# A chain of four modulated convolutions: the last quad's products done in column halves, the row ends' last step on GpSimd, and two steps of VectorE moved in quad 0

## The chip, the cores and the metric

The kernel runs on one core of a Trainium2 chip. The core has TensorE (PE, matrix products into PSUM), VectorE (DVE), ScalarE (ACT), GpSimd (POOL) and SyncE (SP, which here only issues DMAs). The metric is the device time of one launch in microseconds (us). The profile is that of one execution. Its times run from that execution's first instruction, and `L767` is line 767 of the kernel's file.

## The reference

`x` is 128 rows of 64 channels by 1024 positions, and each row has a style vector of 128 numbers. The result is `x` plus four convolutions of three taps in a row (same, upsample with blur, same, downsample with blur), whose weights are modulated and demodulated per row. Cut to what matters:

```python
def _layer(x, style, w, b, mw, mb, typ):
    s = style @ mw.T + mb
    weight = SCALE * w * s[:, None, :, None]
    demod = lax.rsqrt(jnp.sum(weight * weight, axis=(2, 3)) + EPS)
    weight = weight * demod[:, :, None, None]
    if typ == 'same':
        out = jax.vmap(_conv_same)(x, weight) + b[None, :, None]
    elif typ == 'upsample':
        out = jax.vmap(_conv_up)(x, weight.transpose(0, 2, 1, 3)) + b[None, :, None]
        out = _blur(out, 2.0 * blur_k, (1, 1))
    elif typ == 'downsample':
        xb = _blur(x, blur_k, (2, 2))
        out = jax.vmap(_conv_down)(xb, weight) + b[None, :, None]
    return out

out = x
for i, typ in enumerate(('same', 'upsample', 'same', 'downsample')):
    out = _layer(out, style, weights[i], biases[i], mod_w[i], mod_b[i], typ)
return x + out
```

All is float32.

## The kernel before

Away from the ends of a row the four layers and the residual are one linear filter of nine taps, and the kernel builds that filter for every row. Rows are taken four at a time, a **quad**; there are 32 quads, 0 to 31. The 128 partitions hold two rows of 64 channels, and a tile's second axis of two holds the two pairs, so every product on TensorE is a 64x64 weight block against 64 rows of data, four such blocks side by side in the array. A float32 product is issued as two instructions, so that one "product" of a quad below is 3 taps x 4 blocks x 2 = 24 matmul instructions of 340 columns.

For a quad, the weights go through three stages on TensorE (`scale3`, `stage1`, `stage2`, `stage3`; PSUM tiles `psS`, `psR`, `psW`), each copied out with a scale, mostly by ScalarE. The result is `Wf`, with nine taps. The data are cut into three planes, since three neighbouring outputs are computed together by a fast algorithm: five products m0 to m4 in place of nine. VectorE makes three weight sums `H` (`combine_a`: h1, the residual's two small steps at L673, h3; `combine_b`: h2, h1 and h2 once more), and the five data sums `T` (`in_g01` and `in_g2` first make `G`; then `in3` at L725 gives T3, `in1` L740 and `in2` L745 give T12, `in04` L754 gives T04). From quad 1's turn on, `in1` and `in2` of a quad mostly run on GpSimd.

The products add up in PSUM. `conv3` starts the accumulator `psA` with m3; ScalarE copies it out (`copy_m3`, L806); `conv1` adds m1; VectorE forms `y1 = 2*psA + m3` (`sum1`, L676); `conv2` adds m2; `sum2` writes `Y = 3*m3 + psA` into the PSUM tile `Y` (L676) and subtracts psA from y1 (L826); `conv4` adds m4 on top of `Y`; `conv0` adds m0 to psA. The three output planes are psA (0), y1 (1) and Y (2), each times a scale `td` per row and channel, plus a constant `tb` (`output`, L844 on ScalarE, L846 on VectorE). Each plane of 340 columns is stored by a DMA of 170 KB for each pair (L849).

The order of all work is written out by hand: each engine runs its instructions in the order of the program text and waits only for data or for a buffer. Quads 0 to 3 are taken by `early_turn`, 4 to 28 by `turn_of`, and 29, 30 and 31 by straight code at L1509 to L1577. In a turn for quad q the weights of quad q+2 and the data sums of q+1 and q+2 are made beside the products of q and q+1.

The first and last three outputs of each row don't follow the filter. They are worked out in some twenty small steps scattered over the turns into the tile `Oe` (128 partitions x 128 rows x 3). Its last step is `rest3_bias` (L1122): bias and the row's own ends from `Xe` added by VectorE, in two halves of the partitions, in the code of quads 30 and 31, each half followed by a DMA.

Of the kernel before, what the change touches and what calls it, by code (L numbers as in the profile page):

```python
# [63 lines left out]
def kernel(  # L64
# [202 lines left out]
    def var_newton(bs, ls=slice(0, NL)):  # L267

        newton(var[:, ls, bs], dm[:, ls, bs], nw[:, ls, bs])
# [371 lines left out]
    def stage3(q, part, pool=None, engs=(nc_a, nc_a)):  # L641

        t = chain[q]
        ps = unit(pool or ps_w, f"psW{q}_{part}")
        if part == 0:
            new_w(q)
        kinds = ((0, 1), (2,))[part]
        n = 0
        for i, kind in enumerate(kinds):
            for k in range(K):  # L650
                gs = [g for g in range(K) if 0 <= K * g + kind - k < 7]
                lo, m = gs[0], len(gs)
                first = K * lo + kind - k
                n += 1
                step = len(kinds)
                at = slice(i + step * lo, i + step * (lo + m - 1) + 1, step)
                same_row(
                    blocks(ps, at),
                    w0s[kind][:, k, :],
                    t,  # L660
                    slice(first, first + K * (m - 1) + 1, K),
                    n == 1,
                    n == K * len(kinds),
                )
        stage3_out(q, ps, *((3, 6), (0, 3))[part], engs)
        return ps
# [24 lines left out]
    def combine_b(q, steps=range(3)):  # L691

        a, b, c, h1, h2, h3 = taps(q)
        plan = (h2, c, -0.5, a), (h1, b, -3.0, h2, ALU.subtract), (h2, h2, -1.0 / 3.0, b)
        for i in steps:
            sum_of(*plan[i])
# [25 lines left out]
    def in3(q, pairs=BOTH_PAIRS):  # L722
        if q < NQ:
            X, t = Xs[q % NX], t_tile(q, "T3")
            nc_v.tensor_sub(t[:, pairs, 0, :NJ], plane(X, 3, pairs), plane(X, 1, pairs))  # L725
# [16 lines left out]
    def in2(q, eng):  # L742
        if q < NQ:
            t, g = t_tile(q, "T12"), Gs[q]
            eng.tensor_sub(t[:, :, 1, :NJ], plane(g, 2), plane(g, 1))  # L745

    def in04(q, pairs=BOTH_PAIRS):
        if q < NQ:
            t, g = t_tile(q, "T04"), Gs[q]
            a, b = g[:, pairs, :NJ], g[:, pairs, 2 * PL : 2 * PL + NJ]  # L750
            both = lambda v, step: bass.AP(
                v.tensor, v.offset, [*(list(d) for d in v.ap[:-1]), [step, 2], [1, NJ]]
            )
            nc_v.tensor_sub(t[:, pairs, :, :NJ], both(a, PL), both(b, 1))  # L754

    def product(q, m, ps, groups=range(K)):

        W, H_ = Wq[q]
        tag, i = SLOT[m]
        for g in groups:  # L760
            for s, rows in enumerate(HALF):
                for c, cols in enumerate(HALF):
                    if m in (0, 4):
                        w = W[rows, tap(m // 2, g), c, :]
                    else:
                        w = H_[rows, m - 1, g, c, :]
                    nc.tensor.matmul(  # L767
                        ps[s][cols, :NB],
                        w,
                        Ts[q, tag][rows, c, i, g : g + NB],  # L770
                        start=(g == 0 and m == 3),
                        stop=(g == K - 1),
                        skip_group_check=True,
                    )
# [21 lines left out]
    def conv3(q, pool=None):  # L796
        if pool:
            A[q] = unit(pool, f"psA{q}")
        elif q not in A:
            open_a(q)  # L800
        product(q, 3, banks(q))

    def copy_m3(q):
        m3c[q] = m_tile("m3", q)
        for s, a in parts(q):
            nc_a.copy(m3c[q][:, s], a)  # L806
# [10 lines left out]
    def conv2(q, *groups):  # L817
        product(q, 2, banks(q), groups or range(K))
# [9 lines left out]
    def conv4(q, *groups):  # L828
        product(q, 4, Y_banks, groups or range(K))
# [286 lines left out]
                op1=ALU.mult,  # L1116
            )

    def rest3_bias(half):

        rows, xs = ((T, slice(1, 4)), (Bo, slice(4, 7)))[half]
        nc_v.scalar_tensor_tensor(  # L1122
            Oe[rows], Oe[rows], bb[rows, 3:4], Xe[rows, :, xs], op0=ALU.add, op1=ALU.add
        )
        nc.sync.dma_start(out_ends[rows], Oe[rows].rearrange("c b j -> c (b j)"))


    PART = slice(0, 16), slice(16, 32), slice(32, B)
# [200 lines left out]
    def outputs(q, i):  # L1329
        for r in range(2):  # L1330
            output(q, i, r)
            if late(q):
                store(q, r, slice(i, i + 1))

    def early_turn(q):
        n, c, s = q + 1, q + 2, q + 3 + (q >= AHEAD)
        twice = q == AHEAD
        if q == 1:
            nc.sync.dma_start(Xe, x_ends)
        stage2(c)  # L1340
        sum2(q)
        if q == 0:
            in_g01(n)
        if q == 1:
            in_g2(n)
            load(n + NX)
        combine_a(n)
        combine_b(n)
        if q == 0:
            in_g2(n)  # L1350
            load(n + NX)
        conv4(q)
        if q == 0:
            var_matmul(PART[1], var_of(PART[1]), start=False)
            var_root(PART[1], var_of(PART[1]))
            in1(n, nc_v)
            in2(n, nc_v)
            var_newton(PART[1])
            table_A(PART[1], dm[:, 2, PART[1]])
            for of in (table_C, vector_c0, table_3, vector_Da):  # L1360
                of(PART[1])
        if q == 1:
            in1(n, nc_v)
            in2(n, nc_v)
        for i in range(2):
            output(q, 2, i)
        if late(q):
            for i in range(2):
                store(q, i, slice(2, K))
        stage3(c, 0)  # L1370
        conv3(n)
        copy_m3(n)
        extra(q, 0)
        if q in SMALL:
            l, bs = SMALL[q]
            nc_v.memset(high(bs.stop - bs.start), 0.0)
        in04(n)
        if q:
            in3(c)
        if q > 1:  # L1380
            in_g01(c)
        stage3(c, 1)
        conv0(q, 0)
        if q in SMALL:
            small(q)
        if q == 2:
            var_matmul(REST, Y[:, 0], start=(0,))
        conv1(n, 0)
        if twice:
            stage1(s - 1)  # L1390
        else:
            stage1_a(s)
        conv1(n, 1, 2)
        outputs(q, 1)
        if q > 1:
            in_g2(c)
            if q < AHEAD:
                load(c + NX)
        extra(q, 1)
        sum1(n)  # L1400
        if q == 0:
            in3(c)
        if q == 1:
            in_g01(c)
        conv0(q, 1)
        if twice:
            stage1_a(s)
        else:
            stage1_b(s)
        conv0(q, 2)  # L1410
        for i in range(2):
            output(q, 0, i)
        conv2(n, 0)
        if twice:
            stage1_b(s)
        if q == 0:
            in_g01(c)
        if q == 1:
            in_g2(c)
            load(c + NX)  # L1420
        if q:
            in1(c, nc_g)
            in2(c, nc_g)
        extra(q, 2)
        scale3(s + 1)
        if q == AHEAD - 1:
            scale3(s + 2)
        conv2(n, 1, 2)
        for i in range(2):
            store(q, i, slice(0, 1 if late(q) else K))  # L1430
# [79 lines left out]
    stage2(c)  # L1510
    conv2(q)
    in2(n, nc_g)
    stage3(c, 0)
    sum2(q, (0,))
    combine_a(n)
# [15 lines left out]
    combine_b(c, (0,))  # L1531
    conv0(q, 1, 2)
    outputs(q, 0)
    conv2(n)
    sum2(n, (0,))
    combine_b(c, (1,))
# [3 lines left out]
    in2(c, nc_v)  # L1540

    q, n = NQ - 2, NQ - 1
    conv3(n, ps_w)
    copy_m3(n)
    conv4(q, 0, 1)
    for i in range(2):
        output(q, 1, i)
    conv1(n)
    sum1(n)
    conv4(q, 2)  # L1550
    for i in range(2):
        output(q, 2, i)
        store(q, i, slice(1, K))
    in04(n, PAIR[0])
    in04(n, PAIR[1])
    rest3_bias(0)
    conv0(q, 0)
    conv2(n)
    conv0(q, 1, 2)
    sum2(n)  # L1560
    for i in range(2):
        output(q, 0, i)
        store(q, i, slice(0, 1))

    q = NQ - 1
    for i, queue in enumerate((nc.sync, nc_a)):
        output(q, 1, i, nc_v)
        store(q, i, slice(1, 2), queue)
    rest3_bias(1)
    conv4(q)  # L1570
    for i, (eng, queue) in enumerate(zip(BOTH, (nc.sync, nc_a))):
        output(q, 2, i, eng)
        store(q, i, slice(2, K), queue)
    conv0(q, *range(K))
    for i, (eng, queue) in enumerate(zip(BOTH, (nc_a, nc.sync))):
        output(q, 0, i, eng)
        store(q, i, slice(0, 1), queue)  # L1577


# [76 lines left out]
```

## Time and profile before

| | us |
|---|---|
| median of 3 runs | 478.26 (476.77 to 479.97) |
| profiled execution: whole time | 477.31 |
| profiled execution: span of instructions | 475.5 |
| TensorE busy in the span | 469.0 |
| VectorE busy | 418.3 |
| ScalarE busy | 310.6 |
| GpSimd busy | 163.2 |
| last matmul to the end of the span | 4.6 |

The granted TensorE clock was 0.998 of full speed. The views used are the page's busy times; the chain of work that ended last (start, duration, engine, tile, line, count); the timeline of an engine (start, duration, engine, line, operation, output<-inputs, shapes, count, and in brackets how long the engine sat idle before and what it waited for; instructions of one kind that follow each other are merged, "x24"); the groups of instructions by line and shape (count | busy us, mean ns of one | idle before); and the DMA issues (KB, us from issue to landing). Matmul ends are modelled, so that two products in a row overlap by some 0.23 us in the timeline, and the chain shows their spacing.

### The profile page before, as it was taken

The page shows a single profiled execution, that of the slowest core. Times are in us where ns is not written, and L with a number is a line of the kernel's source. Part 1 is how long each engine was busy: PE and PEld are TensorE (multiplying, and loading weights), DVE is VectorE, ACT ScalarE, POOL GpSimd, SP SyncE. Part 2 cuts the span into 40 slices and gives each one's busy share as a digit, 9 for nine tenths or more (in the row PEclk, how much of TensorE's full clock was granted, in tenths as well). Part 3 has the DMA queues.
Part 4 walks back from the last instruction along what each step waited for, and adds up shares of the span by engine and source line. Part 5 has one row for each costly group of instructions (what it writes and reads, how often), then busy time and mean ns, then how long its engine had stood idle before and what let it go on. Part 6 is the DMA issues. An engine that isn't in the chain of part 4 may idle for free.

```text
span 475.5 us, 26756 instructions
## 1 busy us (share of the span) xinstructions
PE 469.0 (99%) x11928; PEld 351.4 (74%) x11928; DVE 418.3 (88%) x693; ACT 310.6 (65%) x709; POOL 163.2 (34%) x197
## 2 busy tenths in 40 slices
PE   8999999999999999999999999999999999999996
PEld 7986788776778877677776677766777788767863
DVE  4889998879989998999979899979999999999895
ACT  5475666668766676766657666667666768766443
POOL 3534032663534342233432233422334432333200
PEclk9999999999999999999999999999999999999999
DMA  5237455545445554345553455544555554455125
GB/s 176 78 108 222 152 160 170 152 132 167 142 139 174 153 177 127 126 145 174 158 156 128 124 167 152 174 128 125 149 175 157 165 157 144 145 145 176 64 91 193
DMA packets 52243, 70.71 MB, mean 149 GB/s; under 512 B 5856, under 2 KB 49824, under 8 KB 52128
## 3 DMA queue, kind: packets, MB, share of 16 engines
q1 hardware_dynamic: 51536, 68.32, 46.4%
q8 instruction: 93, 1.52, 1.4%
q10 hardware_dynamic: 592, 0.69, 0.5%
q14 instruction: 22, 0.18, 0.1%
HBM read 35.36 MB, written 33.62 MB: 145 GB/s over the span
## 4 chain that ended last, share of the span: by engine, by line
PE 94%; DVE 4%; issue 1%; ACT 0%; ACTq 0%; DVEq 0%
PE psA L767 45%; PE Y L767 11%; PE psR L470 9%; PE psA L585 7%; PE psW L585 7%; PE psS L392 5%; PE psR L553 4%; PE psA L470 2%; PE Y L1008 2%; PE Y L339 1%; DVE H L676 1%; PE Y L183 1%; DVE T L754 1%; DVE G L676 0%; PE psM L207 0%
## 5 line engine op out<-in xcount | busy, mean ns | idle before, releaser
L767 PE MATMUL psA<-T,H 64*64 64x340 f32 x2304 | 186.1, 446 | 0.2 <-DVE y L676 0.2
L767 PEld LDWEIGHTS psA<-T,H 64*64 64x64 f32 x2304 | 91.5, 133 | 46.7 <-issue 2.1
L676 DVE SCALAR_TENSOR_TENSOR G<-X 128x1376 f32<-128x1376 f32 (+2 forms) x65 | 78.4, 1212 | 0.2
L740 POOL TENSOR_TENSOR T<-G 128x684 f32<-128x684 f32 x28 | 46.5, 1659 | 74.1 <-DVE G L676 74.1
L448 POOL TENSOR_TENSOR S<-S 128x128 f32<-128x128 f32 x28 | 21.8, 778 | 139.5 <-ACT S L363 132.2
L363 ACT ACTIVATE R<-psR,tC 128x448 f32<-128x448 f32 x63 | 36.6, 631 | 44.7 <-PE psR L470 26.5
L767 PE MATMUL psA<-T,Wf 64*64 64x340 f32 x768 | 64.0, 446 | 0.0
L767 PE MATMUL Y<-T,Wf 64*64 64x340 f32 x768 | 62.6, 451 | 0.1
L676 DVE SCALAR_TENSOR_TENSOR Y<-m,psA 128x340 f32<-128x340 f32 x64 | 33.0, 516 | 27.6 <-PE psA L767 26.2
L363 ACT ACTIVATE psW<-psA 128x128 f32<-128x128 f32 x100 | 19.3, 268 | 49.2 <-PE psA L585 45.1
L754 DVE TENSOR_TENSOR T<-G 128x1368 f32<-128x1368 f32 (+1 forms) x33 | 50.8, 1541 | 0.0
L363 ACT ACTIVATE Wf<-psW,t 128x256 f32<-128x256 f32 (+2 forms) x76 | 32.7, 480 | 26.5 <-PE psW L585 25.6
L725 DVE TENSOR_TENSOR T<-X 128x684 f32<-128x684 f32 x32 | 48.4, 1513 | 0.0
L470 PE MATMUL psR<-S,E 64*64 64x64 f32 (+1 forms) x1472 | 46.9, 237 | 0.0
L745 POOL TENSOR_TENSOR T<-G 128x684 f32<-128x684 f32 x28 | 46.5, 1660 | 0.0
L392 PEld LDWEIGHTS psS<-wd,w2n 64*64 64x64 f32 x1120 | 34.6, 133 | 12.9
L470 PEld LDWEIGHTS psR<-S,E 64*64 64x64 f32 x1472 | 39.5, 134 | 4.9 <-ACT psR L493 0.2
L767 PEld LDWEIGHTS Y<-T,Wf 64*64 64x64 f32 x768 | 30.2, 132 | 17.1 <-DVE Y L676 0.6
L844 ACT ACTIVATE o<-psA,tb,td 128x340 f32<-128x340 f32 x63 | 37.1, 648 | 6.3 <-PE psA L767 6.3
L767 PEld LDWEIGHTS psA<-T,Wf 64*64 64x64 f32 x768 | 30.2, 133 | 13.9
L844 ACT ACTIVATE o<-Y,tb,td 128x340 f32<-128x340 f32 x63 | 36.7, 639 | 4.5 <-PE Y L767 2.7
L844 ACT ACTIVATE o<-y,tb,td 128x340 f32<-128x340 f32 x62 | 38.6, 679 | 0.6 <-DVE y L826 0.6
(165 smaller groups left out, 832.9 us busy)
## 6 DMA issues: line engine op xcount, KB each, us to landing
out<-o SPq DMA_DIRECT2D x185, 170.0 KB, 2.8
X<-in_x SPq DMA_DIRECT2D x150, 172.0 KB, 3.5
X<-in_x SPq DMA_DIRECT2D x14, 516.0 KB, 5.0
out<-o SPq DMA_DIRECT2D x2, 340.0 KB, 2.8
Xe<-in_x_ends SPq DMA_DIRECT2D x1, 512.0 KB, 5.2
out<-o ACTq DMA_DIRECT2D x3, 170.0 KB, 2.7
par<-in_params SPq DMA_DIRECT2D x2, 192.0 KB, 3.6
par<-in_params SPq DMA_DIRECT2D x2, 96.0 KB, 2.6
```

The lines of the kernel that those rows point to most:

```text
L363: nc_a.activation(dst, src, AF.Copy, scale=f)
L392: nc.tensor.matmul(ps[r][cols, at * C : (at + n) * C], weight[rows], wd[c if r == 0 else 1 - c][rows, taps], start=first, stop=last, skip_ ...
L448: nc_g.tensor_add(t[:, :, 2], t[:, :, 2], t[:, :, 0])
L470: nc.tensor.matmul(dst[r][cols], weight[rows], st[c if r == 0 else 1 - c][rows, slots, :], start=False, stop=last, skip_group_check=True,)
L585: nc.tensor.matmul(dst[r][cols], weight[rows], t[rows, c, slots, :], start=first, stop=last, skip_group_check=True,)
L676: nc_v.scalar_tensor_tensor(out, x, f, y, op0=ALU.mult, op1=op)
L725: nc_v.tensor_sub(t[:, pairs, 0, :NJ], plane(X, 3, pairs), plane(X, 1, pairs))
L740: eng.tensor_add(t[:, :, 0, :NJ], plane(g, 2), plane(g, 1))
L745: eng.tensor_sub(t[:, :, 1, :NJ], plane(g, 2), plane(g, 1))
L754: nc_v.tensor_sub(t[:, pairs, :, :NJ], both(a, PL), both(b, 1))
L767: nc.tensor.matmul(ps[s][cols, :NB], w, Ts[q, tag][rows, c, i, g : g + NB], start=(g == 0 and m == 3), stop=(g == K - 1), skip_group_check ...
L844: nc_a.activation(dst, src, AF.Identity, bias=add, scale=d3)
```

## The change

1. **Quad 0's turn.** `combine_b`'s last step for quad 1 (the second h2) moves on VectorE from before `in_g2`, `in1` and `in2` of quad 1 to behind them. `in3(2)` takes the place of `in04(1)`, which moves behind `sum1(1)`.
2. **Row ends.** `rest3_bias` is done by GpSimd in quad 29's code, behind `in2(30)`: one `tensor_scalar` over all of `Oe` (128x384), then two additions of `Xe` (64x384 each, `Xe` taken in runs of 3 of 8). One DMA, `store_ends`, replaces two, and is issued behind quad 29's last outputs. GpSimd then makes three tiny tables (128x2): 2, -1 and 3 times quad 31's `td`.
3. **Quads 30 and 31.** Quad 31's products 3, 1, 2 and 0 are done in two halves of 170 columns, each half with a PSUM tile of its own: right in `ps_w`, left in `ps_conv`. Product 4 stays whole, and starts `Y` by itself (`alone`). On TensorE the order becomes m3 (right, left), quad 30's m4, m1 (right, left), quad 30's m0, m2 (right, left), m4, m0 (left, right). Where the kernel before copied m3 out plainly, ScalarE now makes `m1 = td*m3 + tb` and `m3 = 3*td*m3 + tb`, each in four pieces of 128x170, and VectorE sums with the scales in place: `y1 = 2*td*psA + m1`, plane 1 `= -td*psA + y1`, `m3 = td*psA + m3`, and plane 2 `= td*Y + m3`. So `sum2`'s writing of Y for quad 31 is gone, and planes 1 and 2 need no pass of their own. The left half of plane 0 is scaled by ScalarE and stored while the right half is multiplied; the right half is scaled by ScalarE (pair 0) and VectorE (pair 1) and stored in two DMAs of 85 KB.

The whole diff:

```diff
@@ -753,7 +753,7 @@
             )
             nc_v.tensor_sub(t[:, pairs, :, :NJ], both(a, PL), both(b, 1))
 
-    def product(q, m, ps, groups=range(K)):
+    def product(q, m, ps, groups=range(K), lo=0, hi=NB, alone=False):
 
         W, H_ = Wq[q]
         tag, i = SLOT[m]
@@ -765,10 +765,10 @@
                     else:
                         w = H_[rows, m - 1, g, c, :]
                     nc.tensor.matmul(
-                        ps[s][cols, :NB],
+                        ps[s][cols, : hi - lo],
                         w,
-                        Ts[q, tag][rows, c, i, g : g + NB],
-                        start=(g == 0 and m == 3),
+                        Ts[q, tag][rows, c, i, g + lo : g + hi],
+                        start=(g == 0 and (m == 3 or alone)),
                         stop=(g == K - 1),
                         skip_group_check=True,
                     )
@@ -1116,13 +1116,14 @@
                 op1=ALU.mult,
             )
 
-    def rest3_bias(half):
-
-        rows, xs = ((T, slice(1, 4)), (Bo, slice(4, 7)))[half]
-        nc_v.scalar_tensor_tensor(
-            Oe[rows], Oe[rows], bb[rows, 3:4], Xe[rows, :, xs], op0=ALU.add, op1=ALU.add
-        )
-        nc.sync.dma_start(out_ends[rows], Oe[rows].rearrange("c b j -> c (b j)"))
+    def rest3_bias():
+
+        nc_g.tensor_scalar(Oe, Oe, bb[:, 3:4], None, op0=ALU.add)
+        for rows, xs in ((T, slice(1, 4)), (Bo, slice(4, 7))):
+            nc_g.tensor_add(Oe[rows], Oe[rows], Xe[rows, :, xs])
+
+    def store_ends():
+        nc.sync.dma_start(out_ends, Oe.rearrange("c b j -> c (b j)"))
 
 
     PART = slice(0, 16), slice(16, 32), slice(32, B)
@@ -1345,7 +1346,7 @@
             in_g2(n)
             load(n + NX)
         combine_a(n)
-        combine_b(n)
+        combine_b(n, range(2 if q == 0 else 3))
         if q == 0:
             in_g2(n)
             load(n + NX)
@@ -1355,6 +1356,7 @@
             var_root(PART[1], var_of(PART[1]))
             in1(n, nc_v)
             in2(n, nc_v)
+            combine_b(n, (2,))
             var_newton(PART[1])
             table_A(PART[1], dm[:, 2, PART[1]])
             for of in (table_C, vector_c0, table_3, vector_Da):
@@ -1374,9 +1376,9 @@
         if q in SMALL:
             l, bs = SMALL[q]
             nc_v.memset(high(bs.stop - bs.start), 0.0)
-        in04(n)
         if q:
-            in3(c)
+            in04(n)
+        in3(c)
         if q > 1:
             in_g01(c)
         stage3(c, 1)
@@ -1399,7 +1401,7 @@
         extra(q, 1)
         sum1(n)
         if q == 0:
-            in3(c)
+            in04(n)
         if q == 1:
             in_g01(c)
         conv0(q, 1)
@@ -1510,6 +1512,10 @@
     stage2(c)
     conv2(q)
     in2(n, nc_g)
+    rest3_bias()
+    times = const.tile([P, 3, 2], F32, name="times")
+    for i, f in enumerate((2.0, -1.0, 3.0)):
+        nc_g.tensor_scalar_mul(times[:, i], td[:, c], f)
     stage3(c, 0)
     sum2(q, (0,))
     combine_a(n)
@@ -1531,6 +1537,7 @@
     combine_b(c, (0,))
     conv0(q, 1, 2)
     outputs(q, 0)
+    store_ends()
     conv2(n)
     sum2(n, (0,))
     combine_b(c, (1,))
@@ -1540,41 +1547,78 @@
     in2(c, nc_v)
 
     q, n = NQ - 2, NQ - 1
-    conv3(n, ps_w)
-    copy_m3(n)
-    conv4(q, 0, 1)
+    NH = NB // 2
+    right = unit(ps_w, f"psA{n}")
+    left = ps_conv.tile([P, 2, 512], F32, tag="u", name=f"psA{n}_l")
+    sides = ([left[:, s] for s in range(2)], 0, NH), (right, NH, NB)
+    o = opool.tile([P, 2, K, NB], F32, tag="o", name=f"o{n}")
+    m1, m3, y1 = m_tile("m1", n), m_tile("m3", n), m_tile("y1", n, 2)
+    col = lambda t, i: t[:, i : i + 1]
+    add, one_td = tb[:, n], td[:, n]
+    two_td, minus_td, three_td = (times[:, i] for i in range(3))
+
+    def halved(m, order=(1, 0)):
+        for h in order:
+            product(n, m, sides[h][0], range(K), *sides[h][1:])
+
+    def piece(h, i):
+        ps, lo, hi = sides[h]
+        return (slice(None), i, slice(lo, hi)), ps[i][:, : hi - lo]
+
+    def plus(h, out, f, y):
+        for i in range(2):
+            at, a = piece(h, i)
+            nc_v.scalar_tensor_tensor(out[at], a, col(f, i), y[at], op0=ALU.mult, op1=ALU.add)
+
+    def scaled(h, out, f):
+        for i in range(2):
+            at, a = piece(h, i)
+            nc_a.activation(out[at], a, AF.Identity, bias=col(add, i), scale=col(f, i))
+
+    halved(3)
+    for h in (1, 0):
+        scaled(h, m1, one_td)
+        scaled(h, m3, three_td)
+    conv4(q)
     for i in range(2):
         output(q, 1, i)
-    conv1(n)
-    sum1(n)
-    conv4(q, 2)
+        store(q, i, slice(1, 2))
+    halved(1)
+    plus(1, y1, two_td, m1)
+    in04(n, PAIR[0])
+    plus(0, y1, two_td, m1)
+    in04(n, PAIR[1])
     for i in range(2):
         output(q, 2, i)
-        store(q, i, slice(1, K))
-    in04(n, PAIR[0])
-    in04(n, PAIR[1])
-    rest3_bias(0)
-    conv0(q, 0)
-    conv2(n)
-    conv0(q, 1, 2)
-    sum2(n)
+        store(q, i, slice(2, K))
+    conv0(q, *range(K))
     for i in range(2):
         output(q, 0, i)
         store(q, i, slice(0, 1))
-
-    q = NQ - 1
-    for i, queue in enumerate((nc.sync, nc_a)):
-        output(q, 1, i, nc_v)
-        store(q, i, slice(1, 2), queue)
-    rest3_bias(1)
-    conv4(q)
-    for i, (eng, queue) in enumerate(zip(BOTH, (nc.sync, nc_a))):
-        output(q, 2, i, eng)
-        store(q, i, slice(2, K), queue)
-    conv0(q, *range(K))
-    for i, (eng, queue) in enumerate(zip(BOTH, (nc_a, nc.sync))):
-        output(q, 0, i, eng)
-        store(q, i, slice(0, 1), queue)
+    halved(2)
+    for h in (1, 0):
+        plus(h, o[:, :, 1], minus_td, y1)
+        plus(h, m3, one_td, m3)
+    q, os[n] = n, o
+    for i in range(2):
+        store(q, i, slice(1, 2))
+    product(q, 4, Y_banks, alone=True)
+    for i in range(2):
+        nc_v.scalar_tensor_tensor(
+            o[:, i, 2], Y[:, i, :NB], col(one_td, i), m3[:, i], op0=ALU.mult, op1=ALU.add
+        )
+        store(q, i, slice(2, K))
+    halved(0, (0, 1))
+    scaled(0, o[:, :, 0], one_td)
+    nc.sync.dma_start(out[q, :, :, :NH], o[:, :, 0, :NH])
+    for i, queue in enumerate((nc_a, nc.sync)):
+        at, a = piece(1, i)
+        dst = o[:, :, 0][at]
+        if i:
+            nc_v.tensor_scalar(dst, a, col(one_td, i), col(add, i), op0=ALU.mult, op1=ALU.add)
+        else:
+            nc_a.activation(dst, a, AF.Identity, bias=col(add, i), scale=col(one_td, i))
+        queue.dma_start(out[q, :, i, NH:NB], dst)
 
 
 def kernel(x, cond_512, L0_cond_weights, L0_cond_biases, L0_cond_mod_w, L0_cond_mod_b):
```

## The prediction

> **What bounds the kernel now.** I read the busy times of the page first.
>
> ```profile
> span 475.5 us, 26756 instructions
> PE 469.0 (99%) x11928; PEld 351.4 (74%) x11928; DVE 418.3 (88%) x693; ACT 310.6 (65%) x709; POOL 163.2 (34%) x197
> ```
>
> TensorE is busy for 469.0 of 475.5 us, and the same products remain. So there is little to win: its few stalls, and what follows its last matmul. Next come the last 36 us of the chain, and the last rows of the engines' timelines.
>
> ```profile
> 441.43 1.72 PE psA L767 x24
> 443.15 2.50 PE psR L553 x72
> ...
> 452.32 0.76 PE psW L585 x24
> 453.08 7.07 PE psA L767 x96
> ...
> 466.04 0.50 DVE Y L676
> ```
>
> ```profile
> 467.21 1.95 PE L767 MATMUL Y<-T,Wf 64*64 64x340 f32 x24
> 468.98 1.90 PE L767 MATMUL psA<-T,Wf 64*64 64x340 f32 x24
> 453.06 0.73 ACT L363 ACTIVATE Wf<-psW,t 128x192 f32<-128x192 f32 x2
> 471.13 0.63 ACT L844 ACTIVATE o<-psA,tb,td 128x340 f32<-128x340 f32 x1 [1.08 <-PE psA L767]
> 471.79 0.34 ACTq L849 DMA_DIRECT2D out<-o  x1
> 463.10 0.93 DVE L676 SCALAR_TENSOR_TENSOR y<-psA,m 128x340 f32<-128x340 f32 x2 [0.28 <-PE psA L767]
> ```
>
> A product of 24 instructions takes 1.72 us when nothing waits. The 96 end at 460.15, so quad 31's m3 begins at 460.15 - 1.72 = 458.43. Seven products remain from there: 7 x 1.72 = 12.04, plus the modelled tail of 0.23 (1.95 less 1.72), is 470.70. They really end at 468.98 + 1.90 = 470.88. TensorE thus loses only 0.2 us in the whole end piece. The wait on `sum2` (DVE Y at 466.04), which the change removes, is nearly all hidden by 16 instructions of quad 30's m0. What stands open is the end: one ScalarE output of 0.63 us, a DMA issued at 471.79, and the end of the span at 475.5.
>
> **Part 3, the halves.** Would 170 columns cost half of 340? Per instruction: 1.72/24 = 71.7 ns at 340 columns (0.211 ns a column). The 72 of L553 have 40 of 192 and 32 of 128 columns (nine taps of eight instructions, five taps wide and four narrow), a mean of 163.6 columns, in 2.50/72 = 34.7 ns (0.212 a column). So a half costs 35.9 ns, and 48 of them 1.72 us again. A floor shows below that: L585 at 128 columns takes 0.76/24 = 31.7 ns where the slope gives 27. If its 4.7 ns fell on each of the 4 x 48 half instructions, that were 0.9 us. The L553 row is nearest, so I take **0**, with ends 0 and +0.9.
>
> Do the buffers come free in time? ScalarE has eight copies of 128x170. Two of 192 columns take 0.73, so one costs at most some 0.35 in a run. From the first half's end (458.43 + 0.86 + 0.22 = 459.5) the right side is read by 460.9 and the left by 462.3. Quad 30's m4 stands between, so the halves of m1 want them at 461.87 and 462.73. VectorE's sums of 170 columns cost about 0.3 each (a pair of 340 takes 0.93): two per half after m1, four per half after m2. The last four of the left end about 468.9, and m0's left half wants that buffer at 458.43 + 6 x 1.72 = 468.75. I count 0.1 us of waiting there. m4 of quad 31 waits for nothing new: VectorE ends `in04(31)` some 1.3 us before it. With it TensorE ends at 470.8, **0.1 earlier** than now.
>
> After the last matmul: the right half is one ScalarE copy of some 0.37 us (0.73 for two of 192 columns) in place of 0.63. Now this copy starts 0.25 after TensorE's end, because a DMA issue stands before it on ScalarE; in the new order nothing does, and VectorE's showed a gap of 0.1. So the last DMA is issued at 470.8 + 0.1 + 0.37 = 471.3 in place of 471.79: **-0.5**. It carries 85 KB, not 170.
>
> ```profile
> out<-o SPq DMA_DIRECT2D x185, 170.0 KB, 2.8
> par_s<-in_params_s SPq DMA_DIRECT2D x1, 76.0 KB, 1.9
> ```
>
> The nearest sizes land after 2.8 and 1.9 us, but the second is a read, and 340 KB more of quad 31 is under way. I take **-0.4**, with ends 0 and -0.9. The Trainium skill ("DMA: Bandwidth & Descriptors", the section on the anatomy of one DMA) puts a DMA at about 2.0 us fixed plus bytes over 436 GB/s, for the path issued from GpSimd: by that estimate 85 KB less saves 0.2, and the sum would be 0.2 worse. The -0.4 stands on the two rows.
>
> The end piece gives -0.9, with ends -0.4 and -1.4.
>
> **Part 1, quad 0.** VectorE and TensorE around the two moves:
>
> ```profile
> 35.23 0.56 DVE L676 SCALAR_TENSOR_TENSOR H<-H,Wf 128x384 f32<-128x384 f32 x1
> ...
> 39.31 1.60 DVE L754 TENSOR_TENSOR T<-G 128x1368 f32<-128x1368 f32 x1
> 40.84 0.85 DVE L676 SCALAR_TENSOR_TENSOR y<-psA,m 128x680 f32<-128x680 f32 x1
> ...
> 44.65 1.05 DVE L676 SCALAR_TENSOR_TENSOR Y<-m,psA 128x340 f32<-128x340 f32 x2
> ```
>
> ```profile
> 36.81 0.82 PE L767 MATMUL psA<-T,Wf 64*64 64x340 f32 x8
> 37.62 0.80 PE L767 MATMUL psA<-T,H 64*64 64x340 f32 x8
> ...
> 40.72 0.78 PE L767 MATMUL psA<-T,Wf 64*64 64x340 f32 x8
> 41.74 1.95 PE L767 MATMUL psA<-T,H 64*64 64x340 f32 x24 [0.25 <-DVE y L676]
> ...
> 46.01 1.32 PE L767 MATMUL Y<-T,Wf 64*64 64x340 f32 x16
> ```
>
> Eight instructions are 0.57, so TensorE is free at 37.38 and waits until 37.62 for `in1`, which stands behind h2; and it is free at 41.29 but waits until 41.74 for `sum1`, which stands behind `in04`. With h2 (0.56) behind `in1`, and the short `in3` where `in04` was, both waits go: 0.24 + 0.45 = 0.69. But VectorE's own sum of work up to Y is unchanged, only reordered, so Y still ends about 45.70. m4 of quad 1, now started at 46.01, becomes the next thing late. So only 46.01 - 45.70 = 0.3 is kept: **-0.3**, with ends 0 and -0.7. TensorE has no idle time after that to swallow it.
>
> **Part 2, the row ends.** VectorE loses 2 x 0.6 us of work where it had time. GpSimd gains about 1.25 + 1.0 + 1.0 + 0.6 us right behind `in2(30)`. The prices:
>
> ```profile
> L887 POOL TENSOR_SCALAR w0s<-par 128x192 f32<-128x192 f32 x2 | 1.4, 717 | 2.1 <-DMA par<-in_params 2.1
> L888 POOL TENSOR_SCALAR idn<-par 128x64 f32<-128x64 f32 x1 | 0.4, 361 | 0.0
> ```
>
> (717 - 361)/128 = 2.8 ns an element gives 1.25 us for 384 with a scalar. For an addition of 384 the nearest row is 1.66 us at 684 (443.39, below): 0.93 in proportion, 1.0 with something fixed. No row shows what runs of 3 of 8 cost; that is a rival. The Trainium skill ("GPSIMD Engine Reference", Engine selection) calls one-input work on GpSimd roughly line-rate. By that estimate the first would take some 0.55 us, and the sum would come out 0.7 lower. Here 192 elements took 717 ns, so the trace speaks against it.
>
> GpSimd's time itself is free, but VectorE meets it:
>
> ```profile
> 443.39 1.66 POOL L745 TENSOR_TENSOR T<-G 128x684 f32<-128x684 f32 x1
> 443.26 0.87 DVE L676 SCALAR_TENSOR_TENSOR y<-psA,m 128x680 f32<-128x680 f32 x1 [1.10 <-PE psA L767]
> 444.04 1.74 DVE L725 TENSOR_TENSOR T<-X 128x684 f32<-128x684 f32 x1
> 445.70 1.57 DVE L754 TENSOR_TENSOR T<-G 128x1368 f32<-128x1368 f32 x1
> 447.40 1.07 DVE L676 SCALAR_TENSOR_TENSOR Y<-m,psA 128x340 f32<-128x340 f32 x2
> ...
> 448.85 0.47 DVE L673 SCALAR_TENSOR_TENSOR Wf<-idn,t,Wf 128x64 f32<-128x64 f32 x2
> 449.36 0.56 DVE L676 SCALAR_TENSOR_TENSOR H<-H,Wf 128x384 f32<-128x384 f32 x1
> ...
> 454.55 0.86 DVE L725 TENSOR_TENSOR T<-X 128x684 f32<-128x684 f32 x1
> 455.47 0.87 DVE L676 SCALAR_TENSOR_TENSOR y<-psA,m 128x680 f32<-128x680 f32 x1
> ```
>
> ```profile
> 60.80 1.85 DVE L673 SCALAR_TENSOR_TENSOR Wf<-idn,t,Wf 128x64 f32<-128x64 f32 x2
> ...
> 60.41 1.97 POOL L745 TENSOR_TENSOR T<-G 128x684 f32<-128x684 f32 x1
> ```
>
> The columns are start and duration. `in3` takes 0.86 alone (454.55) but 1.74 beside GpSimd (444.04): it ends 0.73 after GpSimd's op did (445.05), so it stood still until then. A VectorE op with one operand in PSUM doesn't care (443.26 against 455.47). At 60 us the two take turns in the order in which they ask: GpSimd's op first waits for a VectorE step under way (1.97, not 1.66), then L673, asked for later, waits for GpSimd (1.85, not the 0.47 of 448.85).
>
> By that order in quad 29: `in3(30)` until 445.78; then the add over Oe, asked for at 445.0, until about 446.95; then `in04(30)` until 448.45 in place of 447.27; then the first Xe addition until 449.4 beside VectorE's two Y steps, which end at 449.45 in place of 448.47. The second addition holds back h1 until 450.4; h3 is done at about 451.9 in place of 449.92, 2.0 late.
>
> Who waits:
>
> ```profile
> 448.66 1.95 PE L767 MATMUL Y<-T,Wf 64*64 64x340 f32 x24
> 450.37 1.95 PE L767 MATMUL psA<-T,H 64*64 64x340 f32 x24
> ...
> 456.49 3.66 PE L767 MATMUL psA<-T,H 64*64 64x340 f32 x48
> ```
>
> m4 of quad 29 (448.66) needs Y, and m3 of quad 30 (450.37) needs h3: it starts at 451.9, 1.5 late. VectorE runs on without a gap to `sum1(30)` (455.47, ends 456.34), which m2 of quad 30 needs at 456.49, with 0.15 to spare: 2.0 less the slack there is 1.7. After that VectorE has spare time, and everything shifts by **+1.7**. Ends: 0, if the cover at these places is better than I see, and +3.4, if GpSimd's three large ops (1.25 + 2 x 1.0, and 0.15 for the small) all get in ahead of `in04(30)`.
>
> **The sum.** -0.3 + 1.7 - 0.9 + 0 = +0.5 on the profiled execution of 477.31 (its span 475.5 and 1.8 around it): 477.8. That execution lies 0.95 below the median of the three runs, 478.26, which themselves spread over 3.2. I put the sum on the median: **478.7**.
>
> **The rivals.**
>
> *The port wait is hidden* (0.25). The Oe add comes late enough, or the waits fall under VectorE's PSUM steps. For it: VectorE's PSUM step at 443.26 ran beside GpSimd at no cost. Against it: hardly a gap on VectorE between 444 and 456. Then -0.3 - 0.9 = -1.2: 477.1.
>
> *GpSimd holds VectorE longer* (0.14). The place is `in04(30)` at 445.70. If the three large ops go first, or the additions cost half as much again over Xe's short runs, the price is up to +3.4 in place of +1.7, and the sum is +2.2: 480.5, slower than before by 0.5%. It would pass 1% if GpSimd kept `in04(30)` back by about 6 us, that is if the three took twice my price.
>
> *The halves don't run at half price* (0.06). TensorE sits on the floor of 31.7 ns plus some: +0.9, so 479.6.
>
> *The change doesn't do what it says at the end* (0.05): the last DMA lands no sooner, as fixed costs rule, and the left side's buffer holds m0 back: the end gives -0.3, so 479.3.
>
> **The numbers.** The forecast has 0.50. A 1% change is 4.8 us, about what a measurement of this kernel can tell from none. To gain that, the 4.6 us behind the last matmul would have to vanish: 0.01. To lose it takes port waits twice as long: 0.03. All else, 0.96, is within 1%. All low ends together give 478.26 - 0.7 - 1.4 = 476.2, and the longer hold with the floor gives 481.4; a run scatters by 1.5 beside that. The range is 476.2 to 480.9.
>
> **What would show it.** Right: in quad 29 `in04(30)` at over 2.5 us, h1 or h3 of quad 30 stretched to 1 us or more, an idle TensorE ahead of quad 30's m3 and m2; half products 24 instructions in 0.86; the last DMA issued about 0.5 sooner after TensorE's end; quad 1's m4 0.3 earlier. Wrong: no stretched VectorE op behind 445, or halves spaced at 38 ns and more, or VectorE's eight sums after m2 ending behind m4's end, so that m0 waits.

## The result and the profile after

The changed kernel takes 478.57 us in the median (477.04 to 481.05), the kernel before 477.56 (476.44 to 479.97), 22 runs each. The ratio is 1.0024 with a 95% interval of 1.0015 to 1.0033: slower by 1.0 us in the medians, 1.15 by the ratio. The forecast was 478.7, 0.5 above the median then known, in a range of 476.2 to 480.9 and with no change beyond 1%. In what follows a time without a ratio is read from one profiled execution.

The page of the changed kernel, busy times:

```profile
span 476.9 us, 26974 instructions
PE 468.7 (98%) x12024; PEld 348.5 (73%) x12024; DVE 418.8 (88%) x696; ACT 312.9 (66%) x716; POOL 169.8 (36%) x203
```

The span is 1.4 longer and TensorE is busy no longer than before, so its work costs the same, and the 1.4 is waiting and what follows the last matmul. Five marks on TensorE's timeline say where: the start of quad 1's m4, the start of quad 29's m4, the start of quad 30's m2, the last matmul's end, the end of the span. TensorE in the changed kernel:

```profile
46.02 1.90 PE L767 MATMUL Y<-T,Wf 64*64 64x340 f32 x24
...
448.49 1.98 PE L767 MATMUL Y<-T,Wf 64*64 64x340 f32 x23
451.26 1.95 PE L767 MATMUL psA<-T,H 64*64 64x340 f32 x24 [0.79 <-DVE H L676]
...
457.63 2.81 PE L767 MATMUL psA<-T,H 64*64 64x340 f32 x48 [0.22 <-DVE y L676]
...
470.03 1.09 PE L767 MATMUL psA_l<-T,Wf 64*64 64x170 f32 x24
470.95 1.05 PE L767 MATMUL psA<-T,Wf 64*64 64x170 f32 x24
```

| piece | before | after | difference |
|---|---|---|---|
| start to m4 of quad 1 | 46.01 | 46.02 | +0.01 |
| to m4 of quad 29 | 402.65 | 402.47 | -0.18 |
| to m2 of quad 30 | 7.83 | 9.14 | **+1.31** |
| to the end of the last matmul | 14.39 | 14.37 | -0.02 |
| to the end of the span | 4.62 | 4.90 | **+0.28** |

The first piece begins with 0.13 us that is not the change's: quad 1's m3, which stands ahead of the moved steps, starts at 34.47 and not at 34.34. The -0.18 is scatter: this piece took 402.1 to 402.6 us in the traces of the experiments, 402.4 in one whose quad 0 is that of the kernel before (experiment 2). The large item lies between quads 29 and 30. VectorE and GpSimd there:

```profile
443.91 1.63 DVE L725 TENSOR_TENSOR T<-X 128x684 f32<-128x684 f32 x1
445.46 1.57 DVE L754 TENSOR_TENSOR T<-G 128x1368 f32<-128x1368 f32 x1
447.27 1.07 DVE L676 SCALAR_TENSOR_TENSOR Y<-m,psA 128x340 f32<-128x340 f32 x2 [0.24 <-PE psA L767]
448.25 1.27 DVE L676 SCALAR_TENSOR_TENSOR H<-Wf 128x384 f32<-128x384 f32 x1
449.44 1.18 DVE L673 SCALAR_TENSOR_TENSOR Wf<-idn,t,Wf 128x64 f32<-128x64 f32 x2
450.65 0.56 DVE L676 SCALAR_TENSOR_TENSOR H<-H,Wf 128x384 f32<-128x384 f32 x1
```

```profile
444.78 3.29 POOL L1121 TENSOR_SCALAR Oe<-Oe,par_s 128x384 f32<-128x384 f32 x1
448.15 2.19 POOL L1123 TENSOR_TENSOR Oe<-Oe,Xe 64x384 f32<-64x384 f32 x2
```

h1 takes 1.27 us, not 0.55, and the two residual steps 1.18, not 0.47: they stand beside the two additions at 448.15. h3 ends at 451.21 in place of 449.92, and TensorE idles 0.79 ahead of quad 30's m3 and 0.22 ahead of its m2. `in04(30)` at 445.46 is *not* stretched. The trace gives only the start and the end of GpSimd's addition over Oe, 444.78 and 448.07. I read it so: it stood still until `in04(30)` ended at about 447.0, and then took some 1.1 us beside VectorE's Y steps. A row of experiment 1 speaks for this reading.

The end of the changed kernel, on ScalarE, VectorE and SP, and the landing of the last stores:

```profile
471.25 0.88 ACT L1576 ACTIVATE o<-psA_l,tb,td 128x170 f32<-128x170 f32 x2 [3.50 <-PE psA_l L767]
472.03 0.49 ACT L1620 ACTIVATE o<-psA,tb,td 128x170 f32<-128x170 f32 x1
472.09 0.45 DVE L1618 TENSOR_SCALAR o<-psA,td,tb 128x170 f32<-128x170 f32 x1 [0.96 <-PE psA L767]
472.15 0.64 SPq L1613 DMA_DIRECT2D out<-o  x1
472.55 0.35 ACTq L1621 DMA_DIRECT2D out<-o  x1
472.88 0.56 SPq L1621 DMA_DIRECT2D out<-o  x1
```

```profile
out<-o ACTq DMA_DIRECT2D x1, 85.0 KB, 3.0
out<-o SPq DMA_DIRECT2D x1, 85.0 KB, 3.2
```

VectorE's last output is ready at 472.54. Its store is issued at 472.88, since SP is busy for 0.64 us with the store of the left half. The small stores land after 3.0 and 3.2 us, later than the last two of 170 KB in the kernel before, 2.7 each.

### The profile page after: what moved, and what is told of

It reads as the page before. It is cut to its first block, busy times and chain, and to the rows that moved or that the text cites. A ratio compares the mean times of both kernels' runs of the same rounds, so it can differ in the third digit from the quotient of the medians.

```text
span 476.9 us, 26974 instructions
## 1 busy us (share of the span) xinstructions
PE 468.7 (98%) x12024; PEld 348.5 (73%) x12024; DVE 418.8 (88%) x696; ACT 312.9 (66%) x716; POOL 169.8 (36%) x203
## 4 chain that ended last, share of the span: by engine, by line
PE 93%; DVE 4%; DMA 1%; POOL 1%; issue 1%; ACT 0%; SPq 0%; DVEq 0%
PE psA L767 43%; PE Y L767 11%; PE psR L470 9%; PE psA L585 7%; PE psW L585 7%; PE psS L392 5%; PE psR L553 5%; PE psA L470 2%; PE Y L1008 2%; DVE G L676 1%; PE psA_l L767 1%; DMA par_s<-in_params_s 1%; DVE H L676 1%; PE Y L339 1%; DMA out<-o 0%
## 5 line engine op out<-in xcount | busy, mean ns | idle before, releaser
L767 PE MATMUL psA<-T,H 64*64 64x340 f32 (+1 forms) x2304 | 183.0, 442 | 1.0 <-DVE H L676 0.8
L767 PEld LDWEIGHTS psA<-T,H 64*64 64x64 f32 x2304 | 88.2, 133 | 48.4 <-issue 2.7
L767 PE MATMUL psA<-T,Wf 64*64 64x340 f32 (+1 forms) x768 | 62.4, 441 | 0.0
L676 DVE SCALAR_TENSOR_TENSOR Y<-m,psA 128x340 f32<-128x340 f32 x62 | 32.0, 517 | 28.0 <-PE psA L767 26.8
L767 PEld LDWEIGHTS psA<-T,Wf 64*64 64x64 f32 x768 | 28.7, 133 | 14.0
```

The source lines that it names most:

```text
L676: nc_v.scalar_tensor_tensor(out, x, f, y, op0=ALU.mult, op1=op)
L767: nc.tensor.matmul(ps[s][cols, : hi - lo], w, Ts[q, tag][rows, c, i, g + lo : g + hi], start=(g == 0 and (m == 3 or alone)), stop=(g == K ...
```

## The experiments

All times are compared with runs of the kernel before on the same chip, as ratios.

**1. The row ends back on VectorE.** The theory was that GpSimd's reads of SBUF stop VectorE's two-input steps; the rival put the loss in the halved products and the stores.

```diff
     in2(n, nc_g)
-    rest3_bias()
...
-    store_ends()
...
     in04(n, PAIR[1])
+    rest3_bias(0)        # VectorE, 64x384, as in the kernel before
...
         store(q, i, slice(2, K))
+    rest3_bias(1)
+    store_ends()
     halved(0, (0, 1))
```

> The changed kernel, with the row ends' last step taken back from GpSimd to VectorE, in its two gaps of the end piece (0.62 us before quad 31's second product is summed, 0.96 us before the last output); the three tiny tables stay on GpSimd. Theory (GpSimd's work on Oe held VectorE's weight sums of quad 30, and TensorE waited for them): h1 of quad 30 takes 0.55 us again in place of 1.27, its two residual steps 0.47 in place of 1.18, TensorE's idle time ahead of quad 30's m3 and m2 (0.79 and 0.22) is gone, and the time is 1.2 us below the changed kernel's 478.6, so 477.4, even with the kernel before within 0.3. Rival (the loss sits in the halved products and the last stores): the steps may get shorter, but the time stays at 478.3 to 478.8.

Measured: 0.9998 (0.9989 to 1.0008). The steps on VectorE, and TensorE's m3 and m2 of quad 30:

```profile
446.99 0.55 DVE L676 SCALAR_TENSOR_TENSOR H<-Wf 128x384 f32<-128x384 f32 x1
447.45 0.47 DVE L673 SCALAR_TENSOR_TENSOR Wf<-idn,t,Wf 128x64 f32<-128x64 f32 x2
```

```profile
449.00 1.89 PE L767 MATMUL psA<-T,H 64*64 64x340 f32 x24
...
455.09 2.81 PE L767 MATMUL psA<-T,H 64*64 64x340 f32 x48
```

The stretch and the idle brackets are gone, and with them 0.26% or 1.2 us of the changed kernel's time. The two halves on VectorE (0.60 and 0.62) lie in its gaps. GpSimd's three tables of 128x2 now stand where the addition over Oe stood:

```profile
443.64 2.51 POOL L1518 TENSOR_SCALAR times<-td 128x2 f32<-128x2 f32 x3
```

One of the three takes 1.52 us, from 444.44 to 445.97, though it has two columns and another takes 0.21. `in04(30)` runs from 444.32 to 445.89. So a GpSimd op with one tensor input does stand still beside `in04`.

**2. The row ends on GpSimd alone**, on top of the kernel before.

```diff
     in2(n, nc_g)
+    rest3_bias()         # GpSimd, as in the changed kernel
...
+    store_ends()
...
-    rest3_bias(0)
...
-    rest3_bias(1)
```

> The kernel before, with the row ends' last step on GpSimd in quad 29's code as the only change. Theory: the same stretched steps (h1 of quad 30 at about 1.3 us) and the same idle TensorE, less 0.1 for the two additions that VectorE no longer does in the end piece: 1.0 to 1.3 us above the kernel before. Rival: within 0.3 us of the kernel before, since VectorE has 1.2 us less to do.

Measured: 1.0020 (1.0005 to 1.0034), with TensorE waiting for quad 30's h3 again:

```profile
450.90 1.95 PE L767 MATMUL psA<-T,H 64*64 64x340 f32 x24 [0.73 <-DVE H L676]
```

The expectation named the wrong steps: h1 of quad 30 keeps its 0.55 us, and the stretched ones are the residual steps and h3, each by 0.6 to 0.7:

```profile
448.45 1.17 DVE L673 SCALAR_TENSOR_TENSOR Wf<-idn,t,Wf 128x64 f32<-128x64 f32 x2
449.65 1.19 DVE L676 SCALAR_TENSOR_TENSOR H<-H,Wf 128x384 f32<-128x384 f32 x1
```

Within the intervals this part alone gives the whole slowdown, from both sides: taken out of the changed kernel, and put into the one before.

**3. Which order the two engines take.** GpSimd's two-input additions go first:

```diff
-        nc_g.tensor_scalar(Oe, Oe, bb[:, 3:4], None, op0=ALU.add)
         for rows, xs in ((T, slice(1, 4)), (Bo, slice(4, 7))):
             nc_g.tensor_add(Oe[rows], Oe[rows], Xe[rows, :, xs])
+        nc_g.tensor_scalar(Oe, Oe, bb[:, 3:4], None, op0=ALU.add)
```

> The changed kernel, with GpSimd's two additions of Xe ahead of the scalar addition over Oe. Theory 1 (the prediction's: the port goes to whoever asked first, and the scalar addition was passed over because it has one tensor input): the first addition, asked for while in3(30) runs, now gets in ahead of in04(30), which takes 2.5 us in place of 1.57, and TensorE idles ahead of quad 29's m4 too. Theory 2 (a GpSimd op that waits is passed over as long as VectorE's two-input ops follow each other without a gap, whatever the op): in04(30) stays at 1.57, the first addition runs beside the two Y steps that read PSUM, and the stretched ones are h1 or the residual steps as before.

Theory 1 holds for the order, with 2.33 us in place of its 2.5 for `in04(30)`; h1 is not stretched, and quad 29's m4 starts 0.33 us later behind m2 than before. VectorE, then GpSimd:

```profile
445.14 2.33 DVE L754 TENSOR_TENSOR T<-G 128x1368 f32<-128x1368 f32 x1
447.39 1.05 DVE L676 SCALAR_TENSOR_TENSOR Y<-m,psA 128x340 f32<-128x340 f32 x2
448.36 0.55 DVE L676 SCALAR_TENSOR_TENSOR H<-Wf 128x384 f32<-128x384 f32 x1
448.82 0.80 DVE L673 SCALAR_TENSOR_TENSOR Wf<-idn,t,Wf 128x64 f32<-128x64 f32 x2
```

```profile
444.45 3.84 POOL L1122 TENSOR_TENSOR Oe<-Oe,Xe 64x384 f32<-64x384 f32 x2
448.39 1.63 POOL L1123 TENSOR_SCALAR Oe<-Oe,par_s 128x384 f32<-128x384 f32 x1
```

From m2 of quad 29 to m2 of quad 30 TensorE takes 11.07 us in the kernel before, 12.38 in the changed kernel and 11.71 here: the price falls from 1.31 to 0.64. Part of it, as I read it, lies in time that VectorE had until TensorE was done with quad 29's m2 (0.24 us in the changed kernel). The two ops differ in their partitions too, 128 against 64, so that the number of inputs makes the difference is not shown. For this kernel and the next there is no ratio, only the trace.

**4. A GpSimd that is busy, but reads nothing.**

```diff
     in2(n, nc_g)
+    for i in range(9):
+        nc_g.memset(spare, 0.0)      # 128x384; row ends on VectorE
```

> The kernel with the row ends back on VectorE, and nine memsets of 128x384 on GpSimd (about 0.4 us each) where the row ends' step stood: GpSimd as busy as in the changed kernel, but reading nothing. Theory (what VectorE waits for is the read of its second SBUF operand, shared with GpSimd's reads): h1, the residual steps and h3 of quad 30 keep 0.55, 0.47 and 0.56 us, and TensorE doesn't idle there. Rival (any GpSimd instruction in that place holds VectorE): the steps are stretched by 0.4 us at a time.

GpSimd (nine merged), and h1 and the residual steps beside it:

```profile
444.61 4.23 POOL L1518 MEMSET spare<- 128x384 f32 x9
```

```profile
448.15 0.55 DVE L676 SCALAR_TENSOR_TENSOR H<-Wf 128x384 f32<-128x384 f32 x1
448.61 0.48 DVE L673 SCALAR_TENSOR_TENSOR Wf<-idn,t,Wf 128x64 f32<-128x64 f32 x2
```

No step is stretched, and it is 11.10 us between the two m2. So it is not GpSimd's being busy that holds VectorE, but what the row ends' ops do beyond a memset: they read SBUF. The Trainium skill ("SBUF — State Buffer", Who interferes with whom) says so: a VectorE op with two inputs in SBUF contends with GpSimd only where that reads SBUF. This run and the one before agree.

**5. Quad 0 alone.** The kernel before with the two moves of part 1 as in the diff.

> The kernel before, with the two moves in quad 0's turn as the only change. The prediction's step: 0.3 us faster, since Y of quad 1 stays where it was and m4 of quad 1 follows it. Theory after the trace: m1 and m2 of quad 1 come 0.5 us earlier, but GpSimd's addition for quad 3's weights (asked for at about 41, held back by in04 until 42.6) ends at 43.4 as before, so stage 2 of quad 3 starts no earlier: 0.0 to 0.15 us faster, not measurable.

Measured: 0.9998 (0.9983 to 1.0013). From quad 1's m3 to its m4 it is 11.48 us, against 11.67 in the kernel before: a gain of 0.2 in the trace, none that the times can show.

**6. GpSimd's tables later.** On top of the fastest kernel of experiment 7 (row ends on VectorE, whole stores, right half first):

```diff
-            for of in (table_C, vector_c0, table_3, vector_Da):
-                of(PART[1])
...
             stage1_b(s)
+        if q == 0:
+            for of in (table_C, vector_c0, table_3, vector_Da):
+                of(PART[1])
```

> As the one before, and in quad 0's turn GpSimd's four tables for quads 4 to 7 stand behind its addition for quad 3's weights. Theory (that addition, held back by the tables and in04, is why TensorE's earlier m1 and m2 of quad 1 gained nothing): stage 2 of quad 3 starts right behind m2 of quad 1, without the idle 0.35 us, and m4 of quad 1 starts 0.2 to 0.4 us sooner after m3 of quad 1 than in the changed kernel (46.02 - 34.47 = 11.55 us there); the time falls by as much, at the edge of what can be measured. Rival (Y of quad 1 comes last anyway, as the prediction had it): m4 starts within 0.1 us of 11.55 behind m3.

Measured: 0.9980 (0.9963 to 0.9997). In time it can't be told from the kernel it is built on (0.9977), but the trace answers the question. TensorE here, then in the changed kernel (m3, m2, stage 2, m4):

```profile
34.44 1.97 PE L767 MATMUL psA<-T,H 64*64 64x340 f32 x24
...
41.17 1.93 PE L767 MATMUL psA<-T,H 64*64 64x340 f32 x24
42.93 2.87 PE L553 MATMUL psR<-S,E 64*64 64x192 f32 x72
45.56 1.96 PE L767 MATMUL Y<-T,Wf 64*64 64x340 f32 x24
```

```profile
34.47 1.96 PE L767 MATMUL psA<-T,H 64*64 64x340 f32 x24
...
41.20 1.92 PE L767 MATMUL psA<-T,H 64*64 64x340 f32 x24
43.47 2.73 PE L553 MATMUL psR<-S,E 64*64 64x192 f32 x72 [0.35 <-POOL S L448]
```

Behind the tables, stage 2 of quad 3 waited for GpSimd's small addition; ahead of them it starts at once, and m4 comes 11.12 us behind m3, not 11.55 (11.49 in the kernel it is built on). The tables' tiny ops stand still beside `in04(1)`, in the kernel before (first row) as in the changed one (second):

```profile
39.55 1.44 POOL L898 TENSOR_TENSOR c0f<-dm,par_s 128x16 f32<-128x16 f32 x1
```

```profile
40.91 1.80 POOL L287 TENSOR_SCALAR td<-dm 64x8 f32<-64x8 f32 x2
```

The first takes 0.72 in the changed kernel, the second 1.08 in the kernel before. Part 1 moved `in04(1)` from one table to another, and the addition starts 8.48 us behind m3 in the kernel before, 8.50 in the changed one. This is why the earlier m1 and m2 gained so little.

**7. The end piece: its stores and the order of its last halves.** Four kernels. The first has the stores alone changed, on top of the changed kernel:

```diff
     scaled(0, o[:, :, 0], one_td)
-    nc.sync.dma_start(out[q, :, :, :NH], o[:, :, 0, :NH])
...
-        queue.dma_start(out[q, :, i, NH:NB], dst)
+        store(q, i, slice(0, 1), queue)
```

> The changed kernel, with plane 0 of quad 31 stored as two DMAs of 170 KB at the very end, in place of 170 KB after the left half and two of 85 KB after the right. Theory (the last DMA of 85 KB waits 0.34 us for the store of the left half on SP's queue, and DMAs of short rows land 0.3 to 0.5 us later than 170 KB ones): 0.4 to 0.8 us below the changed kernel. Rival (the early store of the left half takes load off the end, as the change has it): 0.2 to 0.5 us above the changed kernel.

Measured: 1.0020 (1.0007 to 1.0032), 0.2 us below the changed kernel's ratio, not the expected 0.4 to 0.8, and not told apart from it, though the span ends 4.13 us after the last matmul and not 4.90. The other three have the row ends back on VectorE. The first of them also does m0 right half first (`halved(0, (1, 0))`, with `scaled(1, ...)` and `piece(0, i)`):

> The kernel with the row ends back on VectorE, plane 0 of quad 31 stored as two whole DMAs of 170 KB, and its product m0 done right half first, so that it doesn't wait for the last two sums of the left half. Theory: the 0.25 us of waiting ahead of m0 goes, the last DMAs are issued together some 0.6 us after the last matmul, and the span ends 4.1 us after it: 0.4 to 0.9 us below the kernel before, ratio 0.998 to 0.9992. Rival (the end piece gives nothing whatever its order): within 0.2 us of the kernel with only the row ends back, ratio 0.9995 to 1.0003.

> The kernel with the row ends back on VectorE, m0 left half first as in the changed kernel, and plane 0 of quad 31 stored as two whole DMAs of 170 KB. The kernel with the row ends back stood at 0.9998 of the kernel before, the one with whole stores and right half first at 0.9977. Theory (the stores are worth 0.7 us, the order of the halves 0.25): ratio 0.9980 to 0.9987, and the span ends about 4.1 us after the last matmul. Rival (the order of the halves is what counts): 0.9995 to 1.0.

> The kernel with the row ends back on VectorE, m0 right half first, and the changed kernel's stores (170 KB of the first half early, two DMAs of 85 KB at the end). Theory (stores 0.7 us, order of the halves 0.25): ratio 0.9990 to 0.9996, the span ends 4.7 to 4.9 us after the last matmul, and TensorE runs from quad 31's m3 to its end in 12.4 us, not 12.65. Rival (the order counts, the stores don't): 0.9975 to 0.9982.

| row ends on VectorE, and | ratio to before | after the last matmul, us |
|---|---|---|
| early store, left first (experiment 1) | 0.9998 (0.9989 to 1.0008) | 4.84 |
| early store, right first | 1.0006 (0.9996 to 1.0017) | 5.37 |
| whole stores, left first | 0.9986 (0.9976 to 0.9996) | 4.34 |
| whole stores, right first | **0.9977** (0.9962 to 0.9993) | 4.32 |

In the traces the whole stores end 0.50 us sooner with the left half first, and 1.05 with the right half first; only in the second pair do the intervals of the ratios lie apart. The kernel with early store and right half first missed its expectation (1.0006 for 0.9990 to 0.9996). With the right half first VectorE's last output waits for ScalarE's, which it does not with the left half first:

```profile
471.43 0.46 DVE L1620 TENSOR_SCALAR o<-psA_l,td,tb 128x170 f32<-128x170 f32 x1 [0.50 <-ACT o L1622]
```

With whole stores and right half first it waits 0.50 too, so that the last two stores are not issued together, as expected, but 0.60 and 1.08 us after the last matmul. There the later one lands after 2.3 us, against 2.9 with the left half first, so that nothing is lost. The issues on SP, with early store and with whole stores (right first both):

```profile
471.38 0.64 SPq L1615 DMA_DIRECT2D out<-o  x1
472.11 0.58 SPq L1623 DMA_DIRECT2D out<-o  x1
```

```profile
471.56 0.33 SPq L849 DMA_DIRECT2D out<-o  x1
```

The stores in rows of 170 columns occupy SP for 0.58 to 0.64 us, those of 340 columns for 0.33. The length of a row can't be all of it: the store of 85 KB issued on ScalarE's queue has rows of 170 columns and takes 0.35. The order of the halves saves 0.25 us on TensorE in the trace (m0 starts 1.71 us behind m4, as a product without a wait does, in place of 1.97), which the times don't separate: 0.9986 and 0.9977 overlap. The last kernel of the table is faster than both kernels of this study.

## Why the prediction was right

The time lies in the range, on the forecast side and far within 1%. That it lies 0.1 us from the forecast is luck: the median that the sum was put on, 478.26, was 0.7 above that of the 22 runs, and the shift is about twice the +0.5 of the sum. The terms erred in both directions: the port (that VectorE and GpSimd wait for each other's reads of SBUF) cost less than forecast, and the end, which should have paid for half of it, cost a little. Of the signs that the prediction named, a stretched h1, an idle TensorE ahead of quad 30's m3 and m2, and (nearly) halves of 0.86 came; `in04(30)` at over 2.5 us, a last DMA 0.5 sooner and a quad 1 0.3 earlier did not, and two signs of being wrong came too: m0 waits, and two of the seven spacings of halves are 0.92 us, 38 ns an instruction.

- **What bounds it:** right, TensorE's busy time hardly changed (469.0 and 468.7). The loss in the kernel before's end piece was misread. The chain's 460.15 is an end that has the tail of 0.23 in it, and the sum added the tail again: quad 31's m3 starts at 458.21, and TensorE loses 0.4 us from there, not 0.2. These 0.4 stand in one place. The 16 instructions at 465.66 take 16 x 0.0717 = 1.15, so m4 could start at 466.81, but waited until 467.21 for `sum2`, which the prediction called nearly all hidden:

```profile
465.66 1.50 PE L767 MATMUL psA<-T,Wf 64*64 64x340 f32 x16
467.21 1.95 PE L767 MATMUL Y<-T,Wf 64*64 64x340 f32 x24
```

The change removed this wait and paid as much for it in the halves and ahead of m0, which gives the -0.02.

- **The halves at half price:** right. 24 instructions of 170 columns start 0.86 to 0.92 us apart (462.81, 463.70 and 464.62, for instance), forecast 0.86. The four products lose about 0.2 us together, forecast 0 with ends 0 and 0.9. ScalarE's copies took 0.38 each in their run of eight, not at most 0.35. The wait ahead of m0 was 0.25, not 0.1.
- **The row ends, +1.7:** the mechanism right, the size 1.31 by the trace and 1.0 to 1.2 by the two ratios. One step of the order failed: "then the add over Oe, asked for at 445.0", ahead of `in04(30)`. It was passed over, and the collisions fell on h1 and the residual steps. With two-input additions first, `in04(30)` is held back as forecast, at a price of 0.64. The price of GpSimd's scalar addition was nearly right: 1.1 by the reading above, for 1.25 us. By the line-rate rule of the Trainium skill ("GPSIMD Engine Reference", Engine selection) an estimate was 0.55; the trace doesn't agree with it.
- **Quad 0, -0.3:** about 0.1 to 0.2 in the traces, none in time. The step "m4 of quad 1, now started at 46.01, becomes the next thing late" overlooked stage 2 before it, which waited for GpSimd's addition. The prediction counted the port in quad 29 and not here, where `in04(1)` stands beside GpSimd's tables before and after the change (experiment 6).
- **The end, -0.9:** wrong, and outside its ends of -0.4 and -1.4; it measured +0.26 (-0.02 and +0.28). The "-0.5" assumed that nothing stands before the last issue. On ScalarE that held (0.55 after the last matmul, against 0.91 before), but the second store stood behind the left half's on SP (0.88). The "-0.4" went by bytes, from a read of 76 KB; the two stores of 85 KB landed later than those of 170, not sooner (in experiment 7 one on ScalarE's queue landed after 1.9). The formula of the Trainium skill ("DMA: Bandwidth & Descriptors", the section on the anatomy of one DMA, for DMAs issued from GpSimd: 2.0 us plus bytes over 436 GB/s) gives an estimate of 2.2 for 85 KB. No DMA here was issued from GpSimd, so no run shows it; these, from SP and ScalarE, took 3.0 and 3.2. Of the rivals, the one on the end (-0.3) came nearest to this term.
- **The rival on a hidden port wait** is out by experiments 1 and 2, that on a longer hold by the trace.

The 0.28 lies behind the last issue: that came 0.88 us after the last matmul, for 0.91 before, and the span ended 4.0 us after it, for 3.7. Open is why these stores land later. Two more traces with the end piece as before (experiment 5, and 2 but for the row ends) end 4.4 us after the last matmul, so 0.2 is scatter here. The stores' gain in time came out as 0.2, 0.6 and 1.4 us by three pairs of ratios, wider than the 0.5 to 1.05 of their traces, though the intervals allow for that.

## What to carry to other kernels

Work put on an idle GpSimd wasn't free here, where its reads met VectorE steps with both inputs in SBUF and TensorE waited for these: look for the stretch of time in which VectorE reads PSUM, or for a gap of VectorE itself, as here. Before a last store is cut in pieces to start earlier, count the issues on its queue and their duration; in the traces two whole stores on two queues ended 0.5 to 1.05 us sooner than three pieces.

## What the runs showed that was not expected

A GpSimd op with one tensor input, asked for while VectorE's two-input ops follow each other, was passed over by the next of them (444.78, ended at 448.07, and the table of two columns that took 1.52 us), while one with two inputs got in between (`in04(30)` at 2.33 us in place of 1.57). And a DMA's issue on SP took 0.64 and 0.56 us for rows of 170 columns against 0.33 for rows of 340, although the one of 0.56 carries half the bytes and a store like it took 0.35 on ScalarE's queue.
